# A gated triangle product and a gated pair layer: the opening and the end in another order

## The chip, the cores and the metric

The kernel runs on one core of one Trainium2 chip. The metric is the device time of one execution in microseconds. Three runs of the kernel before took 3395.56, 3396.61 and 3397.88 us; their median is 3396.61.

## The reference, cut to what matters

The input x is 384 x 384 positions of 128 channels, in fp32. Layer 0:

```
z_n = layernorm(x) * norm_g + norm_b
a   = (z_n Wa + ba) * sigmoid(z_n Wga + bga)
b   = (z_n Wb + bb) * sigmoid(z_n Wgb + bgb)
t   = einsum('ijd,jkd->ikd', a, b)
x   = x + ((layernorm(t) * normo_g + normo_b) Wo + bo) * sigmoid(z_n Wgo + bgo)
```

Layer 1 works on that result, called pair:

```
left  = pair (W_left + W_eq) + b_left + b_eq
right = sum over the row of (pair W_right + b_right)
out   = (left * right * sigmoid(pair W_gate + b_gate)) W_out + b_out
y     = layernorm(out + pair) * ln_scale + ln_bias
```

## The kernel before, in words

The order of instructions on every engine is written out by hand: each engine does its instructions in the order of the program. There are three stages.

**Stage 1** goes over 72 tiles (n) of 128 rows by 16 columns, each in four quarters of four columns. One quarter is one `step(s)`, s = 4n + t, 288 in all. A step multiplies the transposed, normalised quarter zT by four weights (pga, pa, pgb, pb, L201) and, per column, by the weight of the output gate (pgo, L234). ACT takes the sigmoids (L206) and, one step later, the gate's (`gate`, L173); VectorE forms `at` (L218), `bt` (L229) and `gs` (L236). What a step needs of x is made ahead: VectorE takes the statistics of a column (L125, L126), POOL turns them into a factor and an offset with four small operations, one of them a power (`norm_factors`, L132 to L135), ACT normalises four columns (L144), TensorE transposes them (L163), ACT copies them out as zT (L170). In step s ACT normalises the quarter that TensorE reaches three steps later (`ahead`), half of it before the second sigmoid sgb and half after zT. In the first four steps VectorE takes two quarters of statistics ahead of `at`: one of tile 1 and one of tile 2; POOL then works out the factors of tile 1 quarter by quarter. Later steps take one quarter, of the tile after the next, and POOL does the factors of a whole tile at its step t = 0.

POOL also adds the bias b_out to each x tile (`residual`, L154, a sum over 2048 elements a partition) and writes it to Z, and it issues the DMAs of A (L222) and G (L180). SP issues the loads of x (L110; four tiles have room at a time) and of the weights and biases, and the stores of B. Residuals 0, 1 and 2 stand at steps 4, 5 and 6; after step 4 the weight of layer 0's output is made ready (`prepare("o")` with `ob_w`, `center`, `w_o0`, from L309): VectorE and TensorE take turns, and the product `pc` (L314) stands on TensorE ahead of step 5.

Before step 0, `prepare` (L257) transposes each weight, scales it by norm_g on VectorE, and folds norm_b into the bias. The statistics of the four quarters of tile 0 stand between and behind these.

**Stage 2** multiplies 128 channel planes and leaves the sums and sums of squares that normalise t. **Stage 3** goes over the 384 rows u, in groups of R = 4 for loads, factors and stores; a list of stages with lags sets what each iteration does. `norm_factors` (L525) makes the factors of four rows on POOL (12 elements, power at L531), `normalise` (L537) applies them on ACT (L540), and `store` (L569) scales by ln_scale and ln_bias: on POOL for four rows together (L579, L580), but on VectorE row by row (L573, L574) for the last eight rows.

Of the kernel before, what the change touches and what calls it, by code (L numbers as in the profile page):

```python
# [19 lines left out]
def kernel(ctx: ExitStack, tc: tile.TileContext, ins, out: bass.AP):  # L20
# [66 lines left out]

    CG, CX, CT, BR = 64, 16, 4, 32  # L90
    TS = CX // CT
    NT = NB * (N // CX)
    with tc.tile_pool(name="wprep", bufs=6) as wp, tc.tile_pool(name="p1x", bufs=4) as px, tc.tile_pool(name="p1s", bufs=3) as ps, tc.tile_pool(
# [7 lines left out]
            rb, c = divmod(n, N // CX)  # L101
            return rb * P, c * CX

        def fetch(n, parts=1):
            if n >= NT:
                return
            r0, c0 = place(n)
            xt = px.tile([P, CX, C], FP, tag="xt", name=f"xt_{n}")
            for k in range(0, CX, CX // parts):
                nc.sync.dma_start(  # L110
                    out=xt[:, k : k + CX // parts, :], in_=x[r0 : r0 + P, c0 + k : c0 + k + CX // parts, :]
                )
            tiles[n] = {
                "x": xt,
                "st": ps.tile([P, CX, 6], FP, tag="st", name=f"st_{n}"),
                "mv": ps.tile([P, CX, 2], FP, tag="mv", name=f"mv_{n}"),
                "rstd": ps.tile([P, CX], FP, tag="rstd", name=f"rstd_{n}"),
                "off": ps.tile([P, CX], FP, tag="off", name=f"off_{n}"),
            }

        def statistics(n, t):
            if n >= NT:
                return
            for c in range(t * CT, (t + 1) * CT):
                nc.vector.bn_stats(tiles[n]["st"][:, c, :], tiles[n]["x"][:, c, :])  # L125
                nc.vector.bn_aggr(tiles[n]["mv"][:, c, :], tiles[n]["st"][:, c, :])  # L126

# [45 lines left out]
        def gate(s):  # L173
            n, t = divmod(s, TS)
            gs = gated.pop(s)
            gt = tiles[n]["gt"]
            nc.scalar.activation(gt[:, t * CT : (t + 1) * CT, :], gs, AF.Sigmoid)
            if t == TS - 1:
                r0, c0 = place(n)
                nc.gpsimd.dma_start(out=G[r0 : r0 + P, c0 : c0 + CX, :], in_=gt)  # L180
                tiles.pop(n - 1, None)

        def step(s):
            n, t = divmod(s, TS)
            r0, c0 = place(n)
            if t == 0:
                fetch(n + 3)
                if n:
                    norm_factors(n + 1)
                tiles[n]["at"] = po.tile([P, CX, P], FP, tag="at", name=f"at_{n}")  # L190
                tiles[n]["gt"] = po.tile([P, CX, C], FP, tag="gt", name=f"gt_{n}")
                if c0 % CG == 0:
                    bts[n // (CG // CX)] = po.tile([P, P, CG], FP, tag="bt", name=f"bt_{n}")
            at, bt = tiles[n]["at"], bts[n // (CG // CX)]
            k0 = c0 % CG + t * CT
            zT = turned.pop(s)
            ahead = (n + 1, t - 1) if t else (n, TS - 1)

            def proj(k):
                pk = ppp.tile([P, CT, P], FP, tag="pk", name=f"p{k}_{s}")  # L200
                nc.tensor.matmul(pk, lhsT=wT[k], rhs=zT, start=True, stop=True)  # L201
                return pk

            def sigmoid(k, pg):
                sg = ps.tile([P, CT, P], FP, tag="sg", name=f"sg{k}_{s}")
                nc.scalar.activation(sg, pg, AF.Sigmoid, bias=bcol["g" + k])  # L206
                return sg

            if n == 0:
                statistics(1, t)  # L210
                norm_factors(1, t * CT, t * CT + CT)
            statistics(n + 2, t)
            pga, pa = proj("ga"), proj("a")
            sga = sigmoid("a", pga)
            if s:
                gate(s - 1)
            normalise(*ahead, range(CT // 2))
            nc.vector.scalar_tensor_tensor(  # L218
                at[:, t * CT : (t + 1) * CT, :], pa, bcol["a"], sga, ALU.add, ALU.mult
            )  # L220
            if t == TS - 1:
                nc.gpsimd.dma_start(out=A[:, c0 : c0 + CX, r0 : r0 + P], in_=at)  # L222
            pgb = proj("gb")
            sgb = sigmoid("b", pgb)
            turn(s + 1)
            turned_out(s + 1)
            normalise(*ahead, range(CT // 2, CT))
            pb = proj("b")
            nc.vector.scalar_tensor_tensor(  # L229
                bt[:, :, k0 : k0 + CT].rearrange("d r c -> d c r"), pb, bcol["b"], sgb, ALU.add, ALU.mult  # L230
            )
            pgo = ppp.tile([P, CT, C], FP, tag="pk", name=f"pgo_{s}")
            for c in range(CT):
                nc.tensor.matmul(pgo[:, c, :], lhsT=zT[:, c, :], rhs=wT["go"], start=True, stop=True)  # L234
            gs = ps.tile([P, CT, C], FP, tag="gs", name=f"gs_{s}")
            nc.vector.tensor_tensor(gs, pgo, over(gate_bias, CT), ALU.add)  # L236
            gated[s] = gs
            if n == 1 and t < 3:
                residual(t)
            if n > 1 and t == 1:  # L240
                residual(n + 1)
            if k0 + CT == CG:
                b_out_of.extend((bt, r0, c0 + CX - CG, k) for k in range(0, P, BR))
            if t == TS - 1:
                store_b(len(b_out_of) if n == NT - 1 else 1)
# [6 lines left out]
        def weight(k, q):  # L252
            w = wp.tile([P, P], FP, tag="w", name="w_" + k)
            q.dma_start(out=w, in_=ins[L0 + "W" + k])
            wT[k] = w
# [15 lines left out]
                nc.vector.tensor_tensor(bcol[k], pb[:, 0:1], bcol[k], ALU.add)  # L271
            wT[k] = scaled

        fetch(0, TS)
        for k in ("ga", "a", "gb", "b", "go"):
            weight(k, nc.scalar)
        ng, nb = column(L0 + "norm_g"), column(L0 + "norm_b")
        for k in ("ga", "a", "gb", "b"):
            bcol[k] = column(L0 + "b" + k)
        fetch(1)  # L280
        gate_bias = rows(L0 + "bgo")
        fetch(2)
        b_out, b_off = rows(L1 + "b_out"), column(L1 + "b_out")
        og, ob, o_bias = column(L0 + "normo_g"), column(L0 + "normo_b"), rows(L0 + "bo")
# [4 lines left out]
        b_left, b_eq, b_right, b_gate = (column(L1 + k) for k in ("b_left", "b_eq", "b_right", "b_gate"))  # L289
        ln_s, ln_b = rows(L1 + "ln_scale"), rows(L1 + "ln_bias")  # L290

        prepare("ga")
        prepare("a")
        for t in range(TS):
            statistics(0, t)
            norm_factors(0, t * CT, t * CT + CT)
            if t < TS - 1:
                normalise(0, t)
            if t == 0:
                turn(0)  # L300
                turned_out(0)
                prepare("gb")
                prepare("b")
                nc.vector.tensor_copy(nb_w, nb.to_broadcast([P, P]))
            if t == 1:
                prepare("go")
        for s in range(NT * TS):
            step(s)
            if s == TS:  # L309
                nc.vector.tensor_copy(ob_w, ob.to_broadcast([P, P]))  # L310
                prepare("o")
                nc.vector.tensor_scalar(center, ident, -1.0 / C, None, ALU.add)
# [144 lines left out]
    with tc.tile_pool(name="p3s", bufs=4, reuse_waits="tile") as ps, tc.tile_pool(  # L457
# [6 lines left out]
        def of(u):  # L464
            return group[u // R], u % R
# [56 lines left out]
                for q in range(NB):  # L522
                    nc.vector.bn_aggr(b["mv"][:, k, q, :], b["st"][:, k, q, :])

        def norm_factors(u):  # L525
            if u % R:
                return
            g, _ = of(u)
            rs = pg3.tile([P, R, NB], FP, tag="rs1", name=f"rs1_{u}")
            nc.gpsimd.tensor_scalar(rs, g["mv"][:, :, :, 1], EPS, None, ALU.add)  # L530
            nc.gpsimd.tensor_tensor(rs, rs, mhalf[:, 0 : R * NB].rearrange("p (r q) -> p r q", r=R), ALU.pow)  # L531
            off = pg3.tile([P, R, NB], FP, tag="off", name=f"off_{u}")
            nc.gpsimd.tensor_tensor(off, g["mv"][:, :, :, 0], rs, ALU.mult)
            nc.gpsimd.tensor_scalar(off, off, -1.0, None, ALU.mult)  # L534
            g["rs"], g["off"] = rs, off

        def normalise(u):  # L537
            g, i = of(u)
# [28 lines left out]
                nc.scalar.activation(g["right"], pg[:, N : N + R], AF.Identity, bias=b_right)  # L567

        def store(u):  # L569
            if u >= N - 2 * R:  # L570
                g, i = of(u)
                res = g["res"][:, i]
                nc.vector.tensor_tensor(res, res, over(ln_s, NB), ALU.mult)  # L573
                nc.vector.tensor_tensor(res, res, over(ln_b, NB), ALU.add)  # L574
                nc.sync.dma_start(out=y_out[u].rearrange("(p q) c -> p q c", q=NB), in_=res)
            elif u % R == 0:
                g = group.pop(u // R)
                res = g["res"].rearrange("p r q c -> p (r q) c")
                nc.gpsimd.tensor_tensor(res, res, over(ln_s, R * NB), ALU.mult)  # L579
                nc.gpsimd.tensor_tensor(res, res, over(ln_b, R * NB), ALU.add)  # L580
                nc.sync.dma_start(out=y_out[u : u + R].rearrange("i (p q) c -> p i q c", q=NB), in_=g["res"])

        stages = (
            (load, -2 * R), (gate_product, 3), (turn, 2), (out_weights, 7), (layer_1, 8), (layer_0, 0),
            (norm_factors, 12), (normalise, 13), (project, 2), (last_right, 2), (store, 17),
        )
        for u in range(N + stages[-1][1]):
            for stage, lag in stages:
# [41 lines left out]
```

## Time and profile before

| | us |
|---|---|
| median of three runs | 3396.61 |
| the profiled execution | 3399.26 |
| its span | 3397.5 |
| TensorE busy | 3296.4 (97%) |
| VectorE, ACT, POOL busy | 2673.1, 2307.0, 2089.3 |
| step 0, step 1, step 13 start on TensorE (pga, L201) | 20.68, 30.40, 100.23 |
| a step later on | 4.77 |
| stage 2's products start | 1442.55 |
| last instruction of VectorE ends | 3394.53 |

Mean granted TensorE clock: 0.988. In the timeline a row is: start, length, engine, line, operation, output and inputs, and in brackets how long the engine had been idle and what ended it. In the chain of work that ended last a row is start, length and what ran. Times are from the start of the span. A name such as zb is a tile; a count such as x4 is the number of instructions merged.

### The profile page before, as it was taken

How to read it: one execution, taken by the hardware profiler on the slowest of the kernel's cores; microseconds unless marked ns; L12 is line 12 of the kernel's file. 1: busy time of each engine (PE TensorE's matmuls, PEld its weight loads, DVE VectorE, ACT ScalarE, POOL GpSimd, SP SyncE). 2: the span in 40 equal slices, each digit the busy share in tenths (PEclk: the TensorE clock that was granted, in tenths of full speed). 3: DMA queues.
4: the chain of work that ended last, by engine and by line, in shares of the span. 5: the costliest groups of instructions: out<-in, count | busy, mean ns of one | idle time of the engine just before them, and what ended most of it. 6: DMA issues, size and time to landing. Idle time of an engine off the chain costs nothing.

```text
span 3397.5 us, 53333 instructions
## 1 busy us (share of the span) xinstructions
PE 3296.4 (97%) x15581; PEld 2194.5 (65%) x15581; DVE 2673.1 (79%) x8605; ACT 2307.0 (68%) x5482; POOL 2089.3 (61%) x1562
## 2 busy tenths in 40 slices
PE   7999999999999999699999999899999999999997
PEld 4555555555555555355555555478888888888885
DVE  7777777777777777345555555599999999999998
ACT  5777877777877777422222222268888888888887
POOL 5555555555555555245555555338888888888887
PEclk9999999999999999899999999899999999999998
DMA  5888899999988899799999999667777777777773
GB/s 173 263 277 266 261 275 282 279 280 282 285 273 260 266 278 281 217 343 306 302 308 306 304 309 304 215 220 264 264 262 264 264 265 264 265 264 264 265 261 140
DMA packets 675330, 910.52 MB, mean 268 GB/s; under 512 B 319328, under 2 KB 616288, under 8 KB 647520
## 3 DMA queue, kind: packets, MB, share of 16 engines
q1 hardware_dynamic: 634000, 680.28, 63.4%
q0 software_dynamic: 40320, 226.51, 19.1%
q8 instruction: 126, 2.06, 0.2%
q14 instruction: 164, 1.34, 0.1%
q10 hardware_dynamic: 720, 0.33, 0.0%
HBM read 454.04 MB, written 452.98 MB: 267 GB/s over the span
## 4 chain that ended last, share of the span: by engine, by line
PE 91%; DVE 5%; POOL 1%; DMA 1%; issue 1%; SPq 0%; ACT 0%; POOLq 0%; ACTq 0%; DVEq 0%
PE pm L412 20%; PE pgo L234 7%; PE pga L201 7%; PE pa L201 7%; PE pgb L201 7%; PE pb L201 7%; PE pf L497 7%; PE py L507 7%; PE pleft L548 7%; PE pg L550 6%; PE ptr L163 4%; PE ptr L471 3%; DVE py L513 1%; DMA X<-xd 1%; DVE st L518 1%; DVE h L485 1%
## 5 line engine op out<-in xcount | busy, mean ns | idle before, releaser
L412 PE MATMUL pm<-bd,ad 128*128 128x384 f32 x2304 | 748.8, 489 | 32.0 <-DMA bd<-B 32.0
L412 PEld LDWEIGHTS pm<-bd,ad 128*128 128x128 f32 x2304 | 440.2, 191 | 339.2 <-issue 36.9
L427 POOL TENSOR_TENSOR s<-s,xd 128x384 f32<-128x384 f32 x381 | 380.3, 998 | 414.6 <-DVE xd L420 414.3
L425 ACT ACTIVATE sq<-xd 128x384 f32<-128x384 f32 x381 | 188.6, 495 | 566.0 <-DVE xd L420 566.0
L420 DVE TENSOR_TENSOR xd<-pm,x 128x384 f32<-128x384 f32 x381 | 212.2, 557 | 391.0 <-POOL s L427 321.6
L229 DVE SCALAR_TENSOR_TENSOR bt<-pb,c_L_conv_bb,sgb 128x512 f32<-128x512 f32 x288 | 321.0, 1115 | 247.6 <-ACT zT L170 239.1
L144 ACT ACTIVATE zn<-xt,off,rstd 128x128 f32<-128x128 f32 x1152 | 504.4, 489 | 15.1 <-POOL off L135 15.1
L540 ACT ACTIVATE res<-res,off,rs 128x128 f32<-128x128 f32 x1152 | 482.5, 486 | 18.4 <-POOL off L534 15.7
L513 DVE SCALAR_TENSOR_TENSOR py<-py,rs,gr 128x128 f32<-128x128 f32 x1152 | 431.4, 374 | 1.8 <-PE py L507 1.2
L222 POOL DMA_DIRECT2D A<-at x72 | 85.3, 1184 | 552.0 <-DVE at L218 552.0
L206 ACT ACTIVATE sga<-pga,c_L_conv_bga 128x512 f32<-128x512 f32 x288 | 197.9, 687 | 288.2 <-PE pga L201 288.2
L234 PEld LDWEIGHTS pgo<-wT_go,zT 128*128 128x128 f32 x2304 | 302.5, 192 | 137.7 <-issue 72.9
L518 DVE BATCH_NORM_STATS2 st<-res 128x6 f32<-128x128 f32 x1152 | 359.2, 313 | 0.3
L154 POOL TENSOR_TENSOR zb<-xt,r_L_conv_b_out 128x2048 f32<-128x2048 f32 x72 | 327.9, 4554 | 4.4 <-DMA Z<-zb 2.5
L580 POOL TENSOR_TENSOR res<-res,r_L_conv_ln_bias 128x1536 f32<-128x1536 f32 x94 | 324.7, 3455 | 7.4
L497 PE MATMUL pf<-w_o,h 128*128 128x128 f32 x2304 | 321.2, 276 | 6.1 <-ACT w_o L479 5.3
L579 POOL TENSOR_TENSOR res<-res,r_L_conv_ln_scale 128x1536 f32<-128x1536 f32 x94 | 325.4, 3461 | 0.1
L555 ACT ACTIVATE sg<-pg,c_L_conv_b_gate 128x384 f32<-128x384 f32 x384 | 223.0, 581 | 143.8 <-PE pg L550 90.9
L507 PE MATMUL py<-w_o,xr 128*128 128x128 f32 x2304 | 320.4, 275 | 0.0
L548 PE MATMUL pleft<-pairT,m_L_conv_W_left 128*128 128x384 f32 x768 | 313.0, 489 | 1.5 <-ACT pairT L473 1.3
L550 PE MATMUL pg<-pairT,m_L_conv_W_gate 128*128 128x384 f32 x768 | 311.1, 487 | 0.0
L125 DVE BATCH_NORM_STATS2 st<-xt 128x6 f32<-128x128 f32 x1152 | 305.6, 265 | 0.2 <-issue 0.2
(131 smaller groups left out, 6818.9 us busy)
## 6 DMA issues: line engine op xcount, KB each, us to landing
A<-at POOLq DMA_DIRECT2D x72, 1024.0 KB, 7.6
G<-gt POOLq DMA_DIRECT2D x72, 1024.0 KB, 8.8
Z<-zb POOLq DMA_DIRECT2D x72, 1024.0 KB, 8.2
B<-bt SPq DMA_DIRECT2D x72, 1024.0 KB, 16.9
ad<-A SPq DMA_DIRECT2D x128, 576.0 KB, 7.3
bd<-B SPq DMA_DIRECT2D x128, 576.0 KB, 8.2
xr<-X SPq DMA_DIRECT2D x96, 768.0 KB, 6.0
gr<-G SPq DMA_DIRECT2D x96, 768.0 KB, 7.6
```

The lines of the kernel that those rows point to most:

```text
L144: nc.scalar.activation(g["zn"][:, c, :], g["x"][:, c, :], AF.Identity, bias=g["off"][:, c : c + 1], scale=g["rstd"][:, c : c + 1],)
L201: nc.tensor.matmul(pk, lhsT=wT[k], rhs=zT, start=True, stop=True)
L234: nc.tensor.matmul(pgo[:, c, :], lhsT=zT[:, c, :], rhs=wT["go"], start=True, stop=True)
L412: nc.tensor.matmul(pm, lhsT=ad[:, q, ib * P : (ib + 1) * P], rhs=bd[:, q, :], start=(q == 0), stop=(q == NB - 1),)
L427: nc.gpsimd.tensor_tensor(s1[:, ib, :], s1[:, ib, :], xd, ALU.add)
L497: nc.tensor.matmul(pf[:, q, :], lhsT=h[:, q * P : (q + 1) * P], rhs=w_o, start=True, stop=True)
L507: nc.tensor.matmul(py[:, q, :], lhsT=g["x"][:, i, q * P : (q + 1) * P], rhs=w_o0, start=True, stop=True)
L513: nc.vector.scalar_tensor_tensor(py[:, q, :], py[:, q, :], rs0[:, q, u : u + 1], g["g"][:, i, q, :], ALU.mult, ALU.mult)
L518: nc.vector.bn_stats(b["st"][:, k, q, :], b["res"][:, k, q, :])
L540: nc.scalar.activation(g["res"][:, i, q, :], g["res"][:, i, q, :], AF.Identity, bias=g["off"][:, i, q : q + 1], scale=g["rs"][:, i, q : q ...
L548: nc.tensor.matmul(pleft, lhsT=w_left, rhs=pairT, start=True, stop=True)
L550: nc.tensor.matmul(pg[:, 0:N], lhsT=w_gate, rhs=pairT, start=True, stop=True)
```

## The change

Opening: the quarters of tile 0 are loaded one by one between the small loads (`fetch_parts` is a generator). A small activation asks for the sigmoid table before anything else on ACT. The statistics of quarter 0 come before the weights, those of quarters 1, 2 and 3 between them; the third quarter's normalisation moves into step 0. In steps 0 to 11 the statistics of the next tiles stand at the end of the step, behind `gs`, four columns a step and from step 4 on six, and a table says which factors POOL works out in which step. Residuals 0 to 3 stand at steps 3, 6, 8 and 10, and the preparation of "o" moves from after step 4 to after step 12.

End: the last twelve rows instead of eight are scaled on VectorE, with a lag of 20 instead of 17 and behind all statistics; the factors of the last eight rows are made for two rows at a time with a lag of 9 instead of for four with a lag of 12.

```diff
+        FIRST_FACTORS = {
+            0: ((1, 0, 4),), 1: ((1, 4, 8),), 2: ((1, 8, 12),), 3: ((1, 12, 16),),
+            4: ((2, 0, 4),), 5: ((2, 4, 12),), 6: ((2, 12, 16),), 7: ((3, 0, 8),), 9: ((3, 8, 16),),
+        }
+        FIRST_RESIDUALS = {3: 0, 6: 1, 8: 2, 10: 3}
+
+        def first_columns(s):
+            return CX + CT * s + 2 * max(s - TS, 0)
...
-            if n == 0:
-                statistics(1, t)
-                norm_factors(1, t * CT, t * CT + CT)
-            statistics(n + 2, t)
+            if n > 2:
+                statistics((s + 8) * CT, (s + 9) * CT)
...
+            if s == 0:
+                normalise(0, 2)
             normalise(*ahead, range(CT // 2))
...
-            if n == 1 and t < 3:
-                residual(t)
-            if n > 1 and t == 1:
+            if n > 2 and t == 1:
                 residual(n + 1)
+            if n < 3:
+                statistics(first_columns(s), first_columns(s + 1))
+                for m, c0, c1 in FIRST_FACTORS.get(s, ()):
+                    norm_factors(m, c0, c1)
+                if s in FIRST_RESIDUALS:
+                    residual(FIRST_RESIDUALS[s])
...
+        nc.scalar.activation(warm, mhalf, AF.Sigmoid)
...
+        first_quarter(0)
+        normalise(0, 0)
         prepare("ga")
         prepare("a")
-        for t in range(TS):
...
+        turn(0)
+        turned_out(0)
+        first_quarter(1)
+        normalise(0, 1)
+        prepare("gb")
+        prepare("b")
+        first_quarter(2)
+        nc.vector.tensor_copy(nb_w, nb.to_broadcast([P, P]))
+        prepare("go")
+        first_quarter(3)
         for s in range(NT * TS):
             step(s)
-            if s == TS:
+            if s == 3 * TS:
                 nc.vector.tensor_copy(ob_w, ob.to_broadcast([P, P]))
                 prepare("o")
...
+        def norm_factors(u, n=R):
+
+            if u % n or (n == R) != (u < N - 2 * R):
+                return
...
+        def pair_factors(u):
+            norm_factors(u, 2)
...
+        def store_row(u):
+
+            if u < N - 3 * R:
+                return
...
-            (norm_factors, 12), (normalise, 13), (project, 2), (last_right, 2), (store, 17),
+            (norm_factors, 12), (pair_factors, 9), (normalise, 13), (project, 2), (last_right, 2),
+            (store, 17), (store_row, 20),
```

`first_quarter(t)` takes the statistics of four columns of tile 0 and works out their factors. `store_row` does on VectorE, for one row, what `store` did there before (two operations and the row's DMA).

More of the change, by code (lines that the diff above doesn't have):

```diff
@@ L102, in place, with fetch, fetch_parts @@
             return rb * P, c * CX
-        def fetch(n, parts=1):
+        def fetch(n):
+            for _ in fetch_parts(n, 1):
+                pass
+        def fetch_parts(n, parts):
             if n >= NT:
@@ L108, in fetch @@
             xt = px.tile([P, CX, C], FP, tag="xt", name=f"xt_{n}")
[L109 to L112, printed above, removed]
             tiles[n] = {
@@ L119, in fetch, with statistics @@
             }
[L121 to L124, printed above, removed]
+            for k in range(0, CX, CX // parts):
+                nc.sync.dma_start(
+                    out=xt[:, k : k + CX // parts, :], in_=x[r0 : r0 + P, c0 + k : c0 + k + CX // parts, :]
+                )
+                yield
+        def statistics(first, last):
+            for k in range(first, min(last, NT * CX)):
+                n, c = divmod(k, CX)
                 nc.vector.bn_stats(tiles[n]["st"][:, c, :], tiles[n]["x"][:, c, :])
@@ L187, in step @@
                 fetch(n + 3)
-                if n:
+                if n > 2:
                     norm_factors(n + 1)
@@ L207, in sigmoid @@
                 return sg
-            if n == 0:
-                statistics(1, t)
-                norm_factors(1, t * CT, t * CT + CT)
-            statistics(n + 2, t)
+            if n > 2:
+                statistics((s + 8) * CT, (s + 9) * CT)
             pga, pa = proj("ga"), proj("a")
@@ L272, in prepare @@
             wT[k] = scaled
-        fetch(0, TS)
+        warm = wp.tile([P, 16], FP, tag="warm", name="warm", bufs=1)
+        x_parts = fetch_parts(0, TS)
+        next(x_parts)
         for k in ("ga", "a", "gb", "b", "go"):
             weight(k, nc.scalar)
+        nc.scalar.activation(warm, mhalf, AF.Sigmoid)
         ng, nb = column(L0 + "norm_g"), column(L0 + "norm_b")
@@ L279 @@
             bcol[k] = column(L0 + "b" + k)
+            if k in ("a", "b"):
+                next(x_parts)
+        next(x_parts)
+        next(x_parts, None)
+        gate_bias = rows(L0 + "bgo")
         fetch(1)
-        gate_bias = rows(L0 + "bgo")
         fetch(2)
@@ L290, with first_quarter @@
         ln_s, ln_b = rows(L1 + "ln_scale"), rows(L1 + "ln_bias")
+        def first_quarter(t):
+            statistics(t * CT, t * CT + CT)
+            norm_factors(0, t * CT, t * CT + CT)
+        first_quarter(0)
+        normalise(0, 0)
         prepare("ga")
         prepare("a")
-        for t in range(TS):
[L295 to L306, printed above, removed]
+        turn(0)
[8 more added lines that the diff above has]
+        first_quarter(3)
         for s in range(NT * TS):
             step(s)
-            if s == TS:
+            if s == 3 * TS:
                 nc.vector.tensor_copy(ob_w, ob.to_broadcast([P, P]))
@@ L523, in layer_0 @@
                     nc.vector.bn_aggr(b["mv"][:, k, q, :], b["st"][:, k, q, :])
-        def norm_factors(u):
-            if u % R:
+        def norm_factors(u, n=R):
+            if u % n or (n == R) != (u < N - 2 * R):
                 return
[L528 to L533, printed above, removed]
+            g, i = of(u)
+            if i == 0:
+                for k in ("rs", "off"):
+                    g[k] = pg3.tile([P, R, NB], FP, tag=k + "1", name=f"{k}1_{u}")
+            mv, rs, off = (g[k][:, i : i + n] for k in ("mv", "rs", "off"))
+            nc.gpsimd.tensor_scalar(rs, mv[:, :, :, 1], EPS, None, ALU.add)
+            nc.gpsimd.tensor_tensor(rs, rs, mhalf[:, 0 : n * NB].rearrange("p (r q) -> p r q", r=n), ALU.pow)
+            nc.gpsimd.tensor_tensor(off, mv[:, :, :, 0], rs, ALU.mult)
             nc.gpsimd.tensor_scalar(off, off, -1.0, None, ALU.mult)
-            g["rs"], g["off"] = rs, off
+        def pair_factors(u):
+            norm_factors(u, 2)
         def normalise(u):
@@ L569, in store @@
         def store(u):
[L570 to L581, printed above, removed]
+            if u % R or u >= N - 3 * R:
+                return
+            g = group.pop(u // R)
+            res = g["res"].rearrange("p r q c -> p (r q) c")
+            nc.gpsimd.tensor_tensor(res, res, over(ln_s, R * NB), ALU.mult)
+            nc.gpsimd.tensor_tensor(res, res, over(ln_b, R * NB), ALU.add)
+            nc.sync.dma_start(out=y_out[u : u + R].rearrange("i (p q) c -> p i q c", q=NB), in_=g["res"])
+        def store_row(u):
+            if u < N - 3 * R:
+                return
+            g, i = of(u)
+            res = g["res"][:, i]
+            nc.vector.tensor_tensor(res, res, over(ln_s, NB), ALU.mult)
+            nc.vector.tensor_tensor(res, res, over(ln_b, NB), ALU.add)
+            nc.sync.dma_start(out=y_out[u].rearrange("(p q) c -> p q c", q=NB), in_=res)
         stages = (
             (load, -2 * R), (gate_product, 3), (turn, 2), (out_weights, 7), (layer_1, 8), (layer_0, 0),
-            (norm_factors, 12), (normalise, 13), (project, 2), (last_right, 2), (store, 17),
+            (norm_factors, 12), (pair_factors, 9), (normalise, 13), (project, 2), (last_right, 2),
+            (store, 17), (store_row, 20),
         )
```

## The prediction

> **What bounds the kernel now.** I read the chain that ended last first: TensorE carries 91% of it, so a change at the two ends can only move the places where TensorE waits. The change touches neither the 1410 us of projection steps after step 12 nor the products. So I read the chain and the timeline of the first 104 us and of the last 35.
>
> The chain, first 100 us (start, us, what):
> ```profile
> 29.88 0.48 ACT zT L170
> 30.40 2.08 PE pga L201 x2
> ...
> 54.24 0.50 PE w_o L267 x2
> 55.06 4.39 DVE center L312
> 59.58 0.77 PE pc L314 x2
> 60.34 1.71 PE pga L201 x2
> ```
> TensorE starts step 0 at 20.68, step 1 at 30.40 (it waits for zT, which sat behind eight normalisations and a 1.28 us table load on ACT), then runs 4.77 us a step except step 5, which the preparation of "o" holds to 60.14. Step 13 starts at 100.23. Why "center", 0.29 us elsewhere for this size, took 4.4:
> ```profile
> 54.83 4.51 POOL L154 TENSOR_TENSOR zb<-xt,r_L_conv_b_out 128x2048 f32<-128x2048 f32 x1
> ...
> 54.97 4.46 DVE L312 TENSOR_SCALAR center<-ident 128x128 f32<-128x128 f32 x1
> ```
> It began after the residual sum on POOL and ended with it: a hold on DVE. The clock, windows view (us, PE, PEld, DVE, ACT, POOL busy, clock, DMA share, GB/s), shows the second cost, a half clock after the wait:
> ```profile
> 54.00:56.00 2.00, 0.49 (x2) 0.30 (x2) 1.70 (x4) 0.00 (x0) 1.98 (x3) 1.00 0.57 207
> 56.00:58.00 2.00, 0.00 (x0) 0.00 (x0) 2.00 (x1) 0.00 (x0) 2.00 (x1) 0.76 0.95 389
> ```
> The link that will matter, statistics to normalised column (timeline):
> ```profile
> 9.52 0.28 DVE L125 BATCH_NORM_STATS2 st<-xt 128x6 f32<-128x128 f32 x1
> ...
> 11.29 0.23 POOL L132 TENSOR_SCALAR rstd<-mv 128x4 f32<-128x4 f32 x1 [9.93 <-DVE mv L126]
> ...
> 13.29 1.65 ACT L144 ACTIVATE zn<-xt,off,rstd 128x128 f32<-128x128 f32 x4 [7.93 <-POOL off L135]
> ```
> And the end (timeline):
> ```profile
> 3380.84 3.42 POOL L580 TENSOR_TENSOR res<-res,r_L_conv_ln_bias 128x1536 f32<-128x1536 f32 x1
> ...
> 3382.09 2.59 DVE L573 TENSOR_TENSOR res<-res,r_L_conv_ln_scale 128x384 f32<-128x384 f32 x1
> ...
> 3384.87 2.56 POOL L531 TENSOR_TENSOR rs<-rs,mhalf 128x12 f32<-128x12 f32 x1
> 3385.19 0.56 DVE L573 TENSOR_TENSOR res<-res,r_L_conv_ln_scale 128x384 f32<-128x384 f32 x1
> ```
> The last powers start only when POOL has finished scaling four rows (3384.3), though their statistics were done at 3382.2.
>
> **Step 0.** Statistics of the first quarter start when x lands (4.1, where ACT's wait for it ended) instead of 9.52. Two weights prepared (2.2 + 0.3), second quarter's statistics (1.6), two weights (2.4), third quarter (1.6), "go" up to its second product (0.8) follow one after another: step 0 at about 15.5 instead of 20.68. The input's DMAs now stand between small loads on SP, and some wait for a weight to land; the second quarter lands near 8.5 (issue about 5, 3.5 to landing), just when DVE wants it; the others have 2 us or more to spare. The table load moves to about 4.7, in ACT's idle time; worth 1.28 on the path to step 1; the small activation that calls it (0.24 by the nearest, 4 columns wide) is hidden there too. TensorE starts at half clock (before, 1.92 instead of 1.02 until about 22.4)[...]: step 1 at 15.5 + 4.77 + 2 = 22.2 against 30.40, **8.2 ahead**.
>
> **Steps 1 to 12.** Here I expect most of that lead to be given back. Before, the statistics a step takes stand ahead of its "at" and serve the next step's normalisation. Now they stand behind its "gs" and serve the very next step: step 1's first two normalisations stand on ACT ahead of sgb and zT, and wait for powers whose statistics begin after gs of step 0. So a loop: statistics to POOL 1.77 (9.52 to 11.29), POOL to ACT 2.00, two normalisations 0.77, sgb to bt 0.70, bt to gs 0.94, gs to statistics 0.59 (these from steps 1 and 4): **6.8 us** against TensorE's 4.77. Four steps of it: step 5 at 22.2 + 27.1 = 49.3. Step 6: residual 0 now lies on POOL ahead of the first powers of tile 2. POOL takes step 3's powers at 45.3 (2.7 after step 4 starts), then 2.0, residual with its Z issue 5.40 (54.83 to 60.23), G 0.67, the next powers 2.0, and 1.96 from normalisation to pga (28.44 to 30.40): 57.4. Step 7: six statistics instead of four (+0.8) and eight powers instead of four (2.66 by the line through the rows of 4, 12 and 16; +0.6): 8.2 later, 65.6. Then eight columns at once give lead: 4.77 twice, step 9 at 75.1. Step 10 waits again: POOL from 68.7 powers 2.0, residual 1 5.40, A 1.25, eight powers 2.66, so 80.0, and 1.96: 81.9. Then 4.77 twice: step 12 at 91.4 against 95.47, **4.1 ahead**. Tiles 4, 5 and 6 are fetched when residuals 0, 1 and 2 have freed their slots (about 52, 75, 85) and read first at steps 9, 12 and 16: hidden, also for the B stores queued behind them on SP.
>
> **Preparation of "o" after step 12.** The same instructions as before, at another place. DVE now has six statistics of step 11 and four of step 12 in a row (4.0), so gs of step 12 starts near 98.0 and center, 1.80 later as before, at 99.8; pc 0.77; step 13 at 100.4 against 100.23. Unheld it still stops TensorE 4.3 us (step 12's work ends at 96.1), instead of 7.3 and 1.9 of half clock. Opening together: **+0.2**; bounds -6 (clock up at once, a shorter loop) and +4 (clock late in step 0, 1.9 more if it falls in these 4.3 us).
>
> **End.** Pairs of rows 376/377: statistics done 3367.9, four small operations 2.33 (power of 6 by the line through 1.04 for 4 and 2.30 for 12): 3370.3. The scaling of rows 368 to 371 on POOL moves behind them, to 3377.2, hidden: nobody waits but its store. ACT's 3.62 wait at 3377.40 goes, so the weights of row 383 and its statistics are done at 3377.85 instead of 3382.2. Then VectorE is the bound: twelve rows (four more than before) at 1.07 (3385.19 to 3387.33 is two) = 12.84: 3390.7. POOL's last three pairs, 3.3 each beside DVE (the last twelve powers' group took 4.27 there, 3.31 elsewhere), reach 3387.1 and ACT 3389.6: just hidden. Before, DVE ended at 3394.53: **-3.8**, bounds -2 and -5.
>
> [...] The row: behind the 3.42 scaling DVE is indeed held (2.59), but beside the power it ran at 0.55 to 0.56 and POOL paid (2.56 for 2.30). I take the row.
>
> **Sum.** +0.2 - 3.8 = -3.6 on the profiled span of 3397.5 (its execution 3399.26; the median shown, 3396.61, is 2.65 lower and is my base): 3393.0. What a measurement can tell from no change is about 0.2%, 6.8 us.
>
> **Rivals.**
> *The hold comes back (slower than before).* In step 12, POOL's chain from the powers of tile 3 (end 80.0): G 0.67, residual 5.40, powers 2.66, residual 5.40, A 1.25, sixteen powers 3.93, G 0.67: residual 4 starts at 99.9, center at 99.8. If POOL is first by any margin, center ends at 104.5 and the clock falls again: 4.7 + 1.9 = +6.6, **3399.6**. For it: a margin of 0.1 in chains of 20 us. [...]
> *The clock falls in steps 1 to 6.* [...] At 3370 to 3374 it held with 2.2 of 4. [...] At half clock a step is 9.5, 2.7 over the loop: six steps, 16: **3409**.
> *No loop.* If normalisation finds its factors ready, steps run at 4.77: step 12 at 22.2 + 52.5 = 74.7, 16.7 earlier: **3376**. The built order, in which the powers stand behind gs, speaks against it.
>
> **Chances.** Forecast 0.58 (its own range 3389 to 3397), hold 0.22, clock 0.08, no loop 0.12. The range reaches into the last three: 3386 to 3402. Faster by over 0.2%: no loop and a tenth of the forecast, 0.18; slower: half of the clock case and a quarter of the hold, 0.10; within 0.72.
>
> **What would show it.** Step starts (pga) at 15.5, 22, then 6.8 apart to step 5, ACT waiting for POOL's off before each; 75 at step 9; center of 0.3 or of 4.5 us at 99 to 100; one table load; in the end twelve pairs of scaling rows on DVE back to back. Wrong would be: a second quarter of x that lands late, steps 4.77 apart before step 5, or DVE held beside the pairs.

## The result and the profile after

The changed kernel takes 3402.09 us, median of 22 runs (3400.20 to 3403.27); the kernel before, beside it, 3397.53 (22 runs, 3395.20 to 3399.17). That is 4.56 more, a ratio of 1.0014 [1.0008, 1.0020]: slightly slower, where 3.6 less was forecast. The profiled execution took 3400.53 (span 3398.8).

The opening did gain its lead. The timeline shows step 0 at 15.16, step 1 at 21.33 and then starts of 6.8 us apart, each waiting for ACT's zT (start, length, what; in brackets the idle time and what ended it; PE is TensorE, DVE VectorE, ACT ScalarE, POOL GpSimd). ACT in turn waits for POOL's factors, and POOL for VectorE's statistics:

```profile
24.16 0.23 POOL L137 TENSOR_SCALAR rstd<-mv 128x4 f32<-128x4 f32 x1 [4.83 <-DVE mv L131]
...
26.14 0.88 ACT L149 ACTIVATE zn<-xt,off,rstd 128x128 f32<-128x128 f32 x2 [2.44 <-POOL off L140]
...
28.11 1.12 PE L216 MATMUL pga<-zT,wT_ga 128*128 128x512 f32 x2 [1.75 <-ACT zT L175]
...
41.65 1.12 PE L216 MATMUL pga<-zT,wT_ga 128*128 128x512 f32 x2 [1.74 <-ACT zT L175]
...
56.45 1.12 PE L216 MATMUL pga<-zT,wT_ga 128*128 128x512 f32 x2 [2.99 <-ACT zT L175]
...
64.67 1.15 PE L216 MATMUL pga<-zT,wT_ga 128*128 128x512 f32 x2 [3.20 <-ACT zT L175]
...
90.43 1.02 PE L216 MATMUL pga<-zT,wT_ga 128*128 128x512 f32 x2
...
98.80 4.67 DVE L341 TENSOR_SCALAR center<-ident 128x128 f32<-128x128 f32 x1
98.87 4.50 POOL L159 TENSOR_TENSOR zb<-xt,r_L_conv_b_out 128x2048 f32<-128x2048 f32 x1
...
103.62 0.77 PE L343 MATMUL pc<-wT_o,center 128*128 128x128 f32 x2 [5.06 <-DVE center L341]
104.18 1.92 PE L216 MATMUL pga<-zT,wT_ga 128*128 128x512 f32 x2
...
110.15 1.02 PE L216 MATMUL pga<-zT,wT_ga 128*128 128x512 f32 x2
```

Step 12 starts at 90.43, 5.0 before the old 95.47. Then the hold of the old step 4 stands here again: center lasts 4.67 us and ends with the residual sum. Step 13 comes at 104.18 instead of 100.24 and runs at half clock, step 14 at 110.15, where the kernel before has

```profile
105.00 1.02 PE L201 MATMUL pga<-zT,wT_ga 128*128 128x512 f32 x2
```

The lead of 5.0 has become a lag of 5.2. The windows view (us, PE, PEld, DVE, ACT, POOL busy, clock, DMA share, GB/s) shows the clock falling during the hold:

```profile
98.00:101.00 3.00, 0.49 (x2) 0.30 (x2) 2.70 (x4) 0.00 (x0) 2.97 (x3) 0.80 0.97 325
101.00:104.00 3.00, 0.38 (x2) 0.41 (x3) 2.47 (x1) 0.00 (x0) 2.70 (x2) 0.50 0.53 218
104.00:107.00 3.00, 3.00 (x6) 1.38 (x6) 2.35 (x14) 0.87 (x2) 0.25 (x1) 0.57 0.73 306
```

The 0.80 of the first row, 1.8 us at full clock and 1.2 at half, puts the fall, by this estimate, at about 99.8, 1.0 us into the hold. Whether the preparation's own wait ahead of it (2.59 idle before w_o's products at 98.06) has a part in the half clock, no run shows.

The lag is kept to the end of the first stage (its last bt starts at 1414.93 instead of 1409.78) and to the first twelve powers of the end (3368.81 instead of 3363.81). The end wins most of it back (timeline):

```profile
3375.23 3.45 POOL L608 TENSOR_TENSOR res<-res,r_L_conv_ln_scale 128x1536 f32<-128x1536 f32 x1
...
3382.70 0.53 DVE L618 TENSOR_TENSOR res<-res,r_L_conv_ln_scale 128x384 f32<-128x384 f32 x1
...
3385.54 1.62 POOL L564 TENSOR_TENSOR rs<-rs,mhalf 128x6 f32<-128x6 f32 x1
...
3385.86 0.55 DVE L618 TENSOR_TENSOR res<-res,r_L_conv_ln_scale 128x384 f32<-128x384 f32 x1
...
3394.94 0.56 DVE L619 TENSOR_TENSOR res<-res,r_L_conv_ln_bias 128x384 f32<-128x384 f32 x1
```

VectorE scales twelve rows back to back from 3382.70 to 3395.50, 1.07 each, 0.55 beside the power as without it. It ends 1.0 after the last row of VectorE in the kernel before (end 3394.53), although the end began 5.0 later: 4.0 gained.

```profile
3393.97 0.56 DVE L574 TENSOR_TENSOR res<-res,r_L_conv_ln_bias 128x384 f32<-128x384 f32 x1
```

### The profile page after: what moved, and what is told of

Same layout as the page of the kernel before. It is cut to its first block, busy times and chain, and to the rows that moved or that the text cites. A ratio compares the mean times of both kernels' runs of the same rounds, so it can differ in the third digit from the quotient of the medians.

```text
span 3398.8 us, 53367 instructions
## 1 busy us (share of the span) xinstructions
PE 3296.4 (97%) x15581; PEld 2194.3 (65%) x15581; DVE 2671.3 (79%) x8613; ACT 2306.4 (68%) x5482; POOL 2087.7 (61%) x1580
## 4 chain that ended last, share of the span: by engine, by line
PE 94%; DVE 2%; DMA 1%; POOL 1%; ACT 1%; issue 1%; SPq 0%; DVEq 0%; ACTq 0%; POOLq 0%
PE pm L441 21%; PE pf L526 7%; PE py L536 7%; PE pleft L582 7%; PE pgo L249 7%; PE pg L584 7%; PE pga L216 7%; PE pa L216 7%; PE pgb L216 7%; PE pb L216 7%; PE ptr L500 4%; PE ptr L168 4%; DMA X<-xd 1%; SPq L268 0%; DMA B<-bt 0%
## 5 line engine op out<-in xcount | busy, mean ns | idle before, releaser
L542 DVE SCALAR_TENSOR_TENSOR py<-py,rs,gr 128x128 f32<-128x128 f32 x1152 | 383.8, 333 | 1.8 <-PE py L536 1.2
L547 DVE BATCH_NORM_STATS2 st<-res 128x6 f32<-128x128 f32 x1152 | 312.0, 272 | 0.3
L216 PE MATMUL pga<-zT,wT_ga 128*128 128x512 f32 x576 | 297.5, 598 | 13.2 <-ACT zT L175 13.2
```

The lines of the kernel that those rows point to most:

```text
L542: nc.vector.scalar_tensor_tensor(py[:, q, :], py[:, q, :], rs0[:, q, u : u + 1], g["g"][:, i, q, :], ALU.mult, ALU.mult)
```

## The experiments

Theory: two losses in the opening, the loop of 6.8 us that gives most of the lead back, and the hold at step 12; the end gains what was forecast. Rivals: the loss lies elsewhere (a later stage, the spread of runs), or the end's gain isn't real. Each ratio is to the kernel before, timed on the same chip (whose median there was 3397.53 to 3398.15), with its 95% interval:

| kernel | median us | less before | ratio |
|---|---|---|---|
| changed kernel | 3402.09 | +4.6 | 1.0014 [1.0008, 1.0020] |
| e1 center first | 3396.61 | -1.2 | 0.9996 [0.9988, 1.0004] |
| e2 preparation at step 14 | 3394.74 | -3.0 | 0.9992 [0.9984, 1.0000] |
| e3 end alone | 3393.56 | -4.2 | 0.9988 [0.9981, 0.9995] |
| e4 statistics ahead | 3384.59 | -13.2 | 0.9961 [0.9949, 0.9973] |
| e5 both | 3378.33 | -19.8 | 0.9941 [0.9929, 0.9953] |
| e6 opening alone | 3405.33 | +7.2 | 1.0020 [1.0012, 1.0028] |
| e7 old opening, preparation at 14 | 3394.86 | -3.3 | 0.9990 [0.9984, 0.9997] |
| e8 split preparation | 3376.35 | -21.8 | 0.9934 [0.9920, 0.9947] |
| e9 residuals apart | 3388.71 | -9.0 | 0.9975 [0.9965, 0.9986] |
| e10 residuals late | 3379.55 | -18.1 | 0.9946 [0.9933, 0.9960] |

And the starts of steps, from the timelines of the profiled executions:

| step | before | e3 | after | e1 | e2 | e4 | e5 | e7 | e8 | e9 | e10 |
|---|---|---|---|---|---|---|---|---|---|---|---|
| 1 | 30.4 | 30.7 | 21.3 | 22.0 | 21.8 | 21.5 | 22.6 | 30.3 | 21.6 | 30.5 | 21.7 |
| 5 | 60.1 | 58.0 | 48.4 | 49.0 | 48.8 | 40.6 | 41.7 | 51.2 | 40.7 | 50.2 | 40.8 |
| 9 | 81.2 | 79.1 | 76.0 | 74.9 | 74.7 | 61.0 | 62.1 | 70.3 | 61.0 | 69.4 | 59.8 |
| 12 | 95.5 | 93.4 | 90.4 | 91.0 | 90.8 | 75.3 | 76.4 | 90.7 | 75.3 | 83.7 | 74.1 |
| 14 | 105.0 | 102.9 | 110.2 | 104.3 | 100.6 | 93.5 | 85.9 | 100.2 | 84.9 | 95.1 | 86.4 |
| 16 | 114.5 | 112.4 | 119.7 | 115.6 | 113.0 | 103.1 | 98.2 | 112.5 | 94.9 | 107.5 | 98.3 |

**e1, center 1.2 us earlier.**
```diff
             if s == 3 * TS:
+                nc.vector.tensor_scalar(center, ident, -1.0 / C, None, ALU.add)
                 nc.vector.tensor_copy(ob_w, ob.to_broadcast([P, P]))
                 prepare("o")
-                nc.vector.tensor_scalar(center, ident, -1.0 / C, None, ALU.add)
```


> Edit: the changed kernel with center moved to the head of the preparation of "o", some 1.2 us earlier on VectorE; nothing else. Theory (a hold decided by order at step 12): center then runs near 97.6, ahead of the residual sum that starts at 98.87, and takes 0.3 us instead of 4.67; pc near 99.5 and step 13 near 100.2 instead of 104.18. But the 1x128 copy behind pc now falls into the residual sum and may be held to 103.4, so that VectorE and not TensorE is late; part of the 4 to 5 us comes back: 2.5 to 5 less than the changed kernel, 3397 to 3399.5. Rival (the stop is the preparation itself and the clock, the hold is only a label on it): no more than 1 us, 3401 to 3403.

5.5 less than the changed kernel, a little beyond the theory's range. The timeline of e1:

```profile
98.14 0.22 DVE L339 TENSOR_SCALAR center<-ident 128x128 f32<-128x128 f32 x1
...
99.42 4.53 POOL L159 TENSOR_TENSOR zb<-xt,r_L_conv_b_out 128x2048 f32<-128x2048 f32 x1
...
99.48 1.02 PE L216 MATMUL pga<-zT,wT_ga 128*128 128x512 f32 x2
...
99.68 0.29 DVE L344 COPY w_o<-pc 128x128 f32<-128x128 f32 x1
100.00 4.03 DVE L345 COPY w_o<-r_L_conv_bo 1x128 f32<-1x128 f32 x1
```

Center is free (0.22), the copy of pc behind it too (0.29), and the hold falls on the copy of one row (4.03), as expected. TensorE is already in step 13 (99.48 instead of 104.18); the held VectorE costs it 1.7 between steps 14 and 15. By step 16 the changed kernel stands 6.7 behind e2, where nothing is held, and e1 only 2.6: some 4 us of hold cost much less where TensorE doesn't wait for what is held.

**e2, the preparation where GpSimd is idle.**
```diff
-            if s == 3 * TS:
+            if s == 3 * TS + 2:
```


> Edit: the changed kernel with the whole preparation of "o" after step 14 instead of step 12, where GpSimd has nothing to do between 104.3 and 118.5; the same instructions. Theory: nothing of it is held, center 0.3 us, steps 13 and 14 at 95.2 and 100.0, then one stop of about 4.3 us: step 15 at 109.0 instead of 114.92, 5.9 less than the changed kernel: 3396.2 (bounds -4, if the clock falls in that stop, and -6.6). Rival (the 4.6 us between the two kernels were lost elsewhere, in the loop or the later stages): step 15 earlier, but the time within 1.5 us of the changed kernel.

Measured 7.35 less than the changed kernel, more than the 6.6 it allowed. Nothing is held (center takes 0.22; GpSimd has no work from 104.66 to 111.94), and the stop is 108.26 - 100.61 - 4.77 = 2.9 us, not 4.3 (timeline of e2):

```profile
107.60 0.22 DVE L341 TENSOR_SCALAR center<-ident 128x128 f32<-128x128 f32 x1
```

Here VectorE has four statistics a step, not ten in a row: gs, behind which the preparation stands, starts 5.2 us after its step (105.81 in step 14) instead of 6.6 (97.01 in step 12 of the changed kernel).

**e3 and e6, each half alone.** e3 is the old opening with the changed end, e6 the reverse.

> Edit: the opening of the kernel before with the changed end (last three groups scaled by VectorE, last powers by pairs). Theory (the end gained what the sum said, measured 4.0 on VectorE's end against the earlier start of the end): 3.8 less than the kernel before, 3393.7 (3393 to 3394.5). Rival (the end gained only because it started late, or the gain is lost to the store of the last row): 3396.5 to 3397.5. A second rival, VectorE held beside GpSimd's pairs: 3400.7.

> Edit: the changed opening with the end of the kernel before. Theory by the traces (step 14 starts 5.2 later, stages 2 and 3 4.5 to 5.0 later): 4.5 to 5.2 more than the kernel before, 3402.3 to 3403. Theory by the medians (the two kernels differ by 4.6 and the end alone gained 4.2): 8.8 more, 3406.5. Rival (the opening is not the loss, the two halves disturb each other): within 2 us of the kernel before.

The end alone gains 4.2, as forecast. The opening alone costs 7.2, between what traces (5) and medians (8.8) said. The trace of e3 explains part of that gap: its opening is that of the kernel before, but step 2 starts at 35.58, not 38.31. Windows view of the kernel before:

```profile
32.00:34.00 2.00, 2.00 (x4) 0.69 (x3) 1.83 (x11) 1.48 (x3) 0.71 (x2) 0.50 0.00 0
```

and of e3, the same stretch of the same code:

```profile
32.00:34.00 2.00, 2.00 (x9) 1.13 (x8) 1.83 (x11) 2.00 (x5) 0.39 (x2) 1.00 0.00 0
```

The profiled execution of before fell to half clock in step 1, and e3's did not: 2.1 us at step 12. Before's execution lies 1.7 above its median, so "step 12 at 95.47" was a late example, and the lead of 5.0 is 3.0 against e3's 93.4. Why after's execution lies 1.6 below its own median, no trace here tells.

**e4 and e5, the loop broken.** The statistics and factors of steps 0 to 11 go from behind gs to the head of their step; e5 has e2's move as well.
```diff
             if n > 2:
                 statistics((s + 8) * CT, (s + 9) * CT)
+            else:
+                statistics(first_columns(s), first_columns(s + 1))
+                for m, f0, f1 in FIRST_FACTORS.get(s, ()):
+                    norm_factors(m, f0, f1)
             pga, pa = proj("ga"), proj("a")
...
-            if n < 3:
-                statistics(first_columns(s), first_columns(s + 1))
-                for m, c0, c1 in FIRST_FACTORS.get(s, ()):
-                    norm_factors(m, c0, c1)
-                if s in FIRST_RESIDUALS:
-                    residual(FIRST_RESIDUALS[s])
+            if s in FIRST_RESIDUALS:
+                residual(FIRST_RESIDUALS[s])
```


> Edit: the changed kernel with the statistics and factors of steps 0 to 11 issued at the head of their step, ahead of "at", instead of behind "gs"; the preparation of "o" stays after step 12. Theory (the loop of 6.77 us statistics, powers, normalisation, sgb, bt, gs exists only because the statistics stand behind gs): the loop now spans two steps, so TensorE's 4.77 rules: step 5 near 40.4 instead of 48.4 and step 12 near 73.8 instead of 90.4, 16.6 earlier; the stop at step 12 may be 4.3 or 9 us: 3381 to 3386, 16 to 21 less than the changed kernel. Rival (GpSimd's residual sums and powers, or a late x, set the pace of the opening): steps at 5.5 to 6.8, gain under 8 us, 3394 to 3402.

> Edit: both of the two last edits of the opening together (statistics at the head of their step, preparation of "o" after step 14). Theory (the loop and the hold are two separate losses): step 14 at 84.8 as without the move, then one unheld stop of 2.9 us (as measured with the preparation after step 14 alone): step 15 at 92.5 instead of 98.3; 5.9 less than with the statistics alone, 3378.7 (3377 to 3381). Rival (the earlier steps only run ahead into GpSimd's residual sums or into late x tiles, which then set the pace): 3383 to 3386, no gain.

Both came out as the theory said. In e4 the steps follow every 4.77 us to step 5; step 12 is at 75.28 (73.8 expected: step 6 is 1.2 late, its powers stand behind residual 0). e4 still has the hold, now on another operation (timeline of e4):

```profile
80.73 4.51 POOL L159 TENSOR_TENSOR zb<-xt,r_L_conv_b_out 128x2048 f32<-128x2048 f32 x1
...
80.97 4.37 DVE L339 COPY ob_w<-c_L_conv_normo_b 128x128 f32<-128x128 f32 x1
```

e5 takes it away and gains a further 6.3 to 6.7 (4.8 at step 16 of the two profiled executions). The two losses are separate and add up to within about 1 us: against the changed kernel e2 gains 7.4 and e4 17.5, e5 23.8.

**e7, only the old hold taken away.** The old opening, its preparation moved to step 14 as in e2, and the changed end.

> Edit: the opening of the kernel before with its preparation of "o" moved from step 4 to step 14, and the changed end; of the changed opening nothing. Theory (the hold and the half clock behind it, 7.5 and 1.9 us, were all that was to be won there, and an unheld preparation costs 2.9): step 5 at 52.6, step 14 near 95.5, step 15 near 103.2 instead of 109.8: 6.5 less than with the changed end alone, 3387 (3385.5 to 3389). Rival (the preparation costs 4 us or more wherever it stands): 3389 to 3391.

A miss: it gains nothing over e3 (3394.86 against 3393.56). Step 5 starts at 51.2, 6.8 ahead of e3, but step 10 comes at 79.53, 9.24 after step 9 (timeline of e7):

```profile
58.85 4.56 POOL L154 TENSOR_TENSOR zb<-xt,r_L_conv_b_out 128x2048 f32<-128x2048 f32 x1
...
66.89 4.56 POOL L154 TENSOR_TENSOR zb<-xt,r_L_conv_b_out 128x2048 f32<-128x2048 f32 x1 [2.61 <-DMA Z<-zb]
...
73.92 2.94 POOL L133 TENSOR_TENSOR rstd<-rstd,mhalf 128x16 f32<-128x16 f32 x1
...
77.56 0.88 ACT L144 ACTIVATE zn<-xt,off,rstd 128x128 f32<-128x128 f32 x2 [5.00 <-POOL off L135]
79.53 2.08 PE L201 MATMUL pga<-zT,wT_ga 128*128 128x512 f32 x2 [4.31 <-ACT zT L170]
```

GpSimd has three residual sums in a row, the third waiting 2.6 for a buffer, and then tile 3's sixteen powers, for which ACT waits 5.0 us. TensorE, idle for 4.3, comes back at half clock. The hold of the old kernel had covered this wait.

**e9, the residual sums apart.**
```diff
-            if n == 1 and t < 3:
-                residual(t)
-            if n > 1 and t == 1:
+            if s in (4, 6, 9, 11):
+                residual((4, 6, 9, 11).index(s))
+            if n > 2 and t == 1:
                 residual(n + 1)
```


> Edit: the old opening with the preparation at step 14 and the changed end, and GpSimd's residual sums 0 to 3 after steps 4, 6, 9 and 11 instead of 4, 5, 6 and 9. Theory (what took the place of the hold in the old opening is GpSimd: three residual sums in a row, then the sixteen powers of tile 3, which ACT awaited for 5.0 us in step 9, with a half clock behind it): the powers now follow the second sum and the A issue, end near 73.6, ACT waits some 1.1 us, step 10 near 76.2 instead of 79.5 and at full clock: 3 to 5 less than with the sums in a row, 3390 to 3392. Rival (the statistics of tile 3 or its landing were late, not the powers): step 10 stays near 79.5, 3394 to 3396.

5.7 to 6.2 less than e7 (against the kernel before, and by the medians), more than expected: the powers end earlier than thought and ACT no longer waits for them at all (timeline of e9):

```profile
65.01 2.94 POOL L133 TENSOR_TENSOR rstd<-rstd,mhalf 128x16 f32<-128x16 f32 x1
...
76.29 0.87 ACT L144 ACTIVATE zn<-xt,off,rstd 128x128 f32<-128x128 f32 x2
```

One late step is left: residual 3, now after step 11, stands ahead of tile 4's powers, ACT waits 2.4 us for them, and step 14 comes 1.9 late.

So the old opening with two things moved, and the changed end, is 13.4 below the changed kernel.

**e8 and e10, a better version.** e8 is e4 with residual 0 after step 4 instead of 3 and the preparation in two parts, so that no product of it waits for VectorE: transpose, scaling and center after step 14, both products after step 15.
```diff
-        FIRST_RESIDUALS = {3: 0, 6: 1, 8: 2, 10: 3}
+        FIRST_RESIDUALS = {4: 0, 6: 1, 8: 2, 10: 3}
...
+            if s == 3 * TS + 3:
+                both = ppp.tile([P, CT, P], FP, tag="pk", name="pc")
+                pb, pc = both[:, 1, :], both[:, 0, :]
+                nc.tensor.matmul(pb, lhsT=ob_w, rhs=raw, start=True, stop=True)
+                nc.tensor.matmul(pc, lhsT=center, rhs=wT["o"], start=True, stop=True)
```


> Edit: the statistics at the head of their step, residual 0 on GpSimd after step 4 instead of step 3, and the preparation of "o" split over steps 14 and 15, so that TensorE's next work stands ahead of what it waits for on VectorE. Theory: steps 4.77 apart from step 1 (21.5) without a stop but 0.7 for the three small products: step 12 near 74, step 16 near 93.5 (97.2 expected with the preparation in one piece), 3375 (3373.5 to 3377). Rival (VectorE, which has six statistics a step here, is late behind the added operations and TensorE stops all the same): 3377 to 3379.

1.4 above the center of the expectation, because step 7 is still late (5.9 behind step 6); TensorE's stop has shrunk to 0.45 (step 16 at 94.94). e10 then moves the residuals to steps 5, 7, 9 and 11.

> Edit: the best kernel so far (statistics at the head of the step, preparation split over steps 14 and 15) with the residual sums 0 to 3 after steps 5, 7, 9 and 11 instead of 4, 6, 8 and 10, so that none stands ahead of powers that the next step but one needs. Theory: the one late step left (step 7, 5.92 instead of 4.77 apart, ACT waiting for the powers behind residual 0) goes: 1.2 less, 3375.2 (3374.5 to 3376). Rival (x's slots come free later, tile 4 lands after step 9 wants its statistics): a stop at step 9 or 10 instead, 3376 to 3380.

Step 7 is on time now, and yet it is 3.2 to 3.7 slower than e8 (by the medians, and against the kernel before). The rival's time was right, its place and cause were wrong: the stop is at step 14 (timeline of e10):

```profile
74.94 4.55 POOL L159 TENSOR_TENSOR zb<-xt,r_L_conv_b_out 128x2048 f32<-128x2048 f32 x1
...
80.77 2.94 POOL L138 TENSOR_TENSOR rstd<-rstd,mhalf 128x16 f32<-128x16 f32 x1
...
84.40 0.88 ACT L149 ACTIVATE zn<-xt,off,rstd 128x128 f32<-128x128 f32 x2 [3.26 <-POOL off L140]
```

It is not x: residual 3, at step 11, stands ahead of tile 4's sixteen powers, as in e9. Step 14 comes 2.7 us late (86.38), and step 15 a further 1.9, with products at half speed (1.92 and 1.60 for pa and pgb at 87.61 and 89.32, instead of 1.02). The preparation itself is not held. e8 stays the fastest: 25.7 less than the changed kernel (3402.09) and 21.8 less than the kernel before.

## Why the prediction was wrong

The step that failed is the preparation of "o" after step 12. The sum let TensorE stop 4.3 us there, with center free of the residual sum, and step 13 start at 100.4. Center was held for 4.67 us: TensorE stopped 9.0 us, step 13 started at 104.18 and ran at half clock, 1.2 us more.

Taken apart by medians: the end -4.2 (e3), the opening with nothing held and its preparation after step 14 +1.2 (e2 against e3), the hold with the place of the preparation +7.4 (changed kernel against e2; 7.3 by the stops in their traces), together +4.4 of the 4.6 measured. These are steps from one kernel to the next, so their sum is no test of them. e6 and e3 are one: +7.2 and -4.2 make +3.0, so each term is good to some 1.5 us.

- **Step 0 and step 1.** Right: 15.16 and 21.33 for 15.5 and 22.2; one table load, the input in time. The terms named for step 0 add up to 14.6, the first quarter's own statistics (1.6) included; what came on top is a wait of VectorE that the sum left out, 0.6 up to 10.19 for TensorE's transpose of w_gb. That 15.5 came so near is in part luck. Step 0 to step 1 took 6.2 to 7.5 us in the eight executions with this start, so what the slow start costs there (the first product took 1.91 or 1.92 in all eight, 1.02 later; the windows view gives the granted clock as 1.00 from 15 to 21 us of the changed kernel) is a spread, not a number, and the 2 us for it in the sum were my estimate.
- **The loop.** Right, and part by part: 6.77 measured for 6.8 (statistics to POOL 1.77, POOL to ACT 1.98, and so on), step 5 at 48.4 for 49.3. e4 shows that it is the place of the statistics that makes it: with them at the head of the step it is gone.
- **Steps 6 to 12.** Close. The profiled execution lost 1.8 between steps 7 and 8 to a half clock after 3.2 us without work (the clock fell 1.0 us after TensorE had started again, so the row at 64.67 still ran at full speed), and in return step 10 was not late; in e1 and e2 it was the other way round, as forecast (6.5 between steps 9 and 10, 6.8 forecast). Step 12 at 90.4 to 91.0 for 91.4.
- **The preparation of "o".** I put center at 99.8 and residual 4 at 99.9 (its own terms add up to 100.0) and went on with center ahead. They came at 98.80 and 98.87, both about 1.0 early; the margin was 0.07, and by the recorded starts center was even first. It was held all the same. The mechanism and the place of the rival "the hold comes back" were right, and its time near (3.0 over the kernel before forecast, 4.6 measured); what was wrong was giving 0.22 to one side of a race whose margin is less than a hundredth of the two chains that lead to it. e1 shows that a margin of 1.3 us (98.14 to 99.42) is enough. In the kernel before, wT_o, another TENSOR_SCALAR of 128x128, passed in 0.29 us 0.6 ahead of the sum (54.22 to 54.83); between 0.07 and 0.6 no run tells.
- **The price of the hold.** The rival's sum had 4.7 for the hold and 1.9 for the clock. Measured are 4.7 (a stop of 9.0 less the 4.3 forecast unheld) and 1.2. The 7.4 of e2 holds another 1.4: an unheld preparation stops TensorE for 2.9, not 4.3, when it doesn't stand behind ten statistics. The 4.3 itself is not measured; e1, with center out of the way, stops for 3.7 in the same place.
- **The end.** Right: 4.0 on VectorE's last row by the trace, 4.2 by e3, 3.8 forecast. Pairs of powers took 3.2 each beside VectorE (3.3), and VectorE never waited for them. Side by side it was POOL that took longer: a pair's power took 1.35 where it began ahead of VectorE's rows and 1.62 beside them, and the rows stayed at 0.53 to 0.56.
- **The clock in the loop.** It held in the loop (1.75 idle in a row; granted 1.00 from 28 to 49 us), as I had assumed; the case of 3409, in which it falls there, was an estimate. It fell behind stops of 2.6 (e10, step 14), 3.2 (step 7 of the changed kernel) and 4.3 us (e7, step 10). The length of a stop alone doesn't decide it: ahead of step 6 TensorE waited 2.99 us in the changed kernel and kept its clock (1.12 for the first product, 1.00 in the windows view), and the same 2.99 in e1, where the first two products then took 2.08 and 1.72 instead of 1.12 and 1.02 (timeline of e1):

```profile
57.00 2.08 PE L216 MATMUL pga<-zT,wT_ga 128*128 128x512 f32 x2 [2.99 <-ACT zT L175]
```

- **The base.** A profiled execution 1.7 above its median put the old step 12 2.1 us later than in e3. The forecast +0.2 for the opening was a difference from that execution; against e3's step 13 (98.15) the same 100.4 is +2.2.

## What to carry to other kernels

Where an operation of one engine can hold one of another (here a sum on GpSimd center on VectorE, 4.67 us for 0.22), a margin of 0.1 us at the end of chains of 20 us is not a margin: price both sides, and place the operation where the other engine has nothing to do. A lead is worth only as much as the next resource grants: look which engine is late once the wait is gone (here GpSimd's powers behind a residual sum, 5.0 us of ACT's waiting in e7), and put work that feeds the next steps ahead of work that only stores. Work that was taken ahead helped when it stood before the step's own waits in its queue (4.77 us a step in e4); behind them it turned a pipeline into a loop (6.77).

## What was not expected of the hardware

- The recorded start doesn't tell who won: center's row begins 0.07 before the residual sum's (98.80 and 98.87), and yet it lasts as long as the whole sum (to 103.47 and 103.37). In e6, with the sum at 98.85, step 13 again starts only at 104.15.
- The same residual sum held a copy of one row of 128 numbers from SBUF for 4.03 us, and let a 128x128 copy out of PSUM, just before it, pass in 0.29 (e1). The kernel before has this second hold too, 4.13 us at 60.71 behind residual 1, and the prediction did not read it.
- The clock of the same instructions differed from one execution to the next (0.50 and 1.00 at 32 to 34 us). Step 6 of the changed kernel and of e1 differs in the same way, behind the same 2.99 us of waiting (1.12 and 2.08 for its first product). What decides it, no run here shows.
